# A four-layer graph network: TensorE's order given in the source, sums over features in quarters of columns, aggregation in 64x64 tiles

## The chip, the cores and the metric

The kernel runs on one core of one Trainium2 chip. A core has five engines with queues of their own: TensorE (PE in the profile, with its weight loads shown as PEld), VectorE (DVE), ScalarE (ACT), GpSimd (POOL) and SyncE (SP), which here only starts transfers. Matmul results land in PSUM, eight banks of 512 float32 values per partition; everything else lives in SBUF, 128 partitions wide. The metric is the device time of one execution in microseconds, the median of several runs.

## What is computed

The input x has 128 graphs of 64 nodes with 256 features, in float32. Four layers follow each other, each `x = layernorm(x + layer(x, adj))`:

```python
# layer 0: attention over the adjacency
Wh = x @ W
e = leaky(Wh @ a1 [:, None] + Wh @ a2 [None, :]);  e = -inf where adj == 0
out0 = softmax(e) @ Wh
# layer 1: attention over 512 edges (src, dst), 4 heads of 64 features
Xq, Xv = x @ W_lin.T, x @ W_val.T
e = einsum('behd,hd->beh', leaky_relu(Xq[:, src] + Xq[:, dst], 0.2), a) + log(A0[src, dst] + EPS)
attn = softmax of e over the edges with the same src
out1 = segment_sum(attn * Xv[:, dst], src) @ W_out.T
# layer 2: normalised adjacency, then two dense layers with batch norms
agg = A_hat @ x;  out2 = batchnorm(relu(batchnorm(agg @ W1.T + b1)) @ W2.T + b2)
# layer 3: two graph convolutions, then four LSTMs over windows of 1 to 4 nodes
```

Layers 0 and 1 and the first step of layer 2 (`agg`) are what the change touches.

## The kernel before

The 8192 rows (graph, node) are handled in sixteen blocks q of 512 rows, which is 8 graphs, or 4 columns c of 128 rows with 2 graphs (s) each. While block q is in the edge scores of layer 1, block q+2 is in layer 0, block q+1 is prepared for layer 1, and block q-3 gets its values, output projection and aggregation. Tiles in PSUM are `m` (three banks), `z` (two times two banks) and `e` (one bank).

The edge scores use leaky(t) = 0.2 t + 0.8 relu(t). The weights |a| are folded into the query weights, so that the sum over a head's features only has signs left. Per graph b of a block, one matmul pair z gathers query + query for all 512 edges (256 features in two halves of 128), ScalarE takes relu, VectorE adds the two halves (with a sign `same`, as the features are permuted so that both halves hold the same heads), and a matmul with the one-column-per-head matrix `apad` sums over features into 4 of the 128 rows of `e`:

```python
def reduce_heads(q, b, t):                                   # L312
    ...
    r0 = ((s * BPS + q % BPS) * PQ + c) * HEADS
    nc.tensor.matmul(pes[S], apad[:, P - HEADS - r0:2 * P - HEADS - r0], t, start=first, stop=False)

def l1_graph(q, b):
    c, s = divmod(b, 2)
    z = bank([KD, E], name="z", bufs=2)
    for k in range(KD):                                      # L322
        nc.tensor.matmul(z[:, k, :], L1[q]["qs"][c][:, s, k * P:(k + 1) * P], gath_r, start=True, stop=True)
    u = work.tile([P, KD, E], F32, name="u", bufs=4)
    nc.scalar.activation(u, z, AF.Relu)                      # L324
    nc.vector.scalar_tensor_tensor(u[:, 0, :], u[:, 1, :], same, u[:, 0, :], op0=OP.mult, op1=OP.add)  # L325
    pend.append((q, b, u[:, 0, :]))
    if len(pend) > DEEP:
        reduce_heads(*pend.pop(0))
```

Every second block, the softmax over edges runs on VectorE over the filled `e` (16 graphs x 4 heads in rows), with scans for the maximum and the sum per source node. Its result is scattered to a table in DRAM and read back (`ld`):

```python
def l1_softmax(S):
    nc.tensor.matmul(pe, spads[S % 2], gath, start=False, stop=True)                                 # L335
    nc.vector.tensor_add(e, pe, lb)
    nc.vector.tensor_tensor_scan(up, seg[:, :E], e, NEG, OP.add, OP.max)
    nc.vector.tensor_tensor_scan(dn[:, ::-1], seg[:, 1:][:, ::-1], e[:, ::-1], NEG, OP.add, OP.max)
    nc.vector.tensor_max(up, up, dn)
    nc.vector.tensor_sub(e, e, up)
    nc.scalar.activation(e, e, AF.Exp)
    ...  # two more scans; transposes of e and dn (L353); reciprocal (L357); weights at (L359); scatter; read back
```

Values, output projection and the aggregation for layer 2:

```python
def v_a(q):          # values: 64x64 tiles
    ...
    for c in range(PQ):
        for h in range(HEADS):
            for s in range(2):                               # L384
                nc.tensor.matmul(pY[s][r0:r0 + 64, h // 2, c, :], v[r, c, h * 64:(h + 1) * 64],
                                 am[r, c * HEADS + h, :], start=True, stop=True)
def v_b(q): ...      # output projection (L398), addition, layernorm into x2 on GpSimd, x2 to DRAM
def v_c(q):          # aggregation, with the block-diagonal matrix aht of two graphs
    for k in range(KD):
        p_ = bank([PQ, P])
        for c in range(PQ):                                  # L410
            nc.tensor.matmul(p_[:, c, :], x2[:, c, k * P:(k + 1) * P], aht, start=True, stop=True)
        nc.scalar.activation(A[:, q, k * QT:(k + 1) * QT], p_.rearrange("p c t -> p (c t)"), AF.Copy)
```

The loop names the steps in a rough order; what stands where on each engine is then settled by a scheduler that builds the program:

```python
for q in range(NQ):
    between = [
        [(l0_a, q + 2)],                      # transposes of x                (L201)
        [(l0_b, q + 2), (v_a, q - LAG)],      # layer 0's projection           (L222)
        [(l0_c, q + 2)],                      # scores, mask, exponentials     (L233, L236, L244)
        [(v_b, q - LAG), (l1_t, q + 1)],      # l1_t: transposes for layer 1   (L201)
        [(l1_qv, q + 1, 0), (l0_d, q + 2)],   # queries L287, values L290
        [],
        [(l1_qv, q + 1, 1), (v_c, q - LAG)],
        [(l0_e, q + 2)],                      # layer 0's aggregation (L263), layernorm
    ]
    for b in range(GQ):
        some(l1_graph, q, b)
        if q and q % BPS == 0 and b == DEEP - 1:
            l1_softmax(q // BPS - 1)
        for step, n, *more in between[b]:
            some(step, n, *more)
```

After the loop, the last three blocks' v_a, v_b and v_c alternate with layer 2's blocks (`up_block`, L684); layer 2's second dense layer is L749, layer 3's LSTMs are L927 and L933.

Of the kernel before, what the change touches and what calls it, by code (L numbers as in the profile page):

```python
# [17 lines left out]
P = 128  # L18
NB = 128
N = 64  # L20
# [11 lines left out]
SROWS = BPS * GQ * HEADS  # L32
PAIRS = N * N
# [7 lines left out]
def kernel(ctx: ExitStack, tc: tile.TileContext, i, out):  # L41
# [42 lines left out]
    def layernorm(dst, src, n, engine):  # L84
# [3 lines left out]
        ng = small.tile([P, n], F32, name="ln_ng", bufs=6)  # L88
        rs = small.tile([P, n], F32, name="ln_rs", bufs=6)
# [21 lines left out]
    with ExitStack() as two:  # L111
# [52 lines left out]
        for k in range(KD):  # L164
            for m in range(KD):
                nc.scalar.dma_start(
                    wq[:, k, m * P:(m + 1) * P].rearrange("p (h j) -> p h j", h=HEADS),
                    i["W_linT"][k * P:(k + 1) * P].rearrange("p (h m j) -> p m h j", h=HEADS, m=KD)[:, m])
        aL1 = su.tile([P, D], F32, name="aL1")
        for m in range(KD):  # L170
            nc.scalar.dma_start(aL1[:, m * P:(m + 1) * P].rearrange("p (h j) -> p h j", h=HEADS),
                              i["L1_gnn_a"].rearrange("h (m j) -> m h j", m=KD)[m].partition_broadcast(P))
# [4 lines left out]
        apad = wa.tile([P, 2 * P - HEADS], F32, name="apad")  # L177
        same = wa.tile([P, 1], F32, name="same")
# [37 lines left out]
        def l0_b(q):  # L216
# [10 lines left out]
            nc.gpsimd.tensor_copy(sb, wh[:, :, D + 1:].to_broadcast([P, PQ, P]))  # L227

        def l0_c(q):
# [4 lines left out]
            t = own(q, [P, PQ, P], "lr")  # L234
            for c in range(PQ):
                nc.vector.scalar_tensor_tensor(t[:, c, :], sc[:, c, :], wh[:, c, D:D + 1], mask,  # L236
                                               op0=OP.add, op1=OP.add)
            e = L0[q]["e"] = work.tile([P, PQ, P], F32, name="e0")
            nc.vector.scalar_tensor_tensor(e, t, SLOPE, t, op0=OP.mult, op1=OP.max)
# [40 lines left out]
        def l1_qv(q, c2):  # L280
            xT, v = L1[q]["xT"], L1[q]["v"]
            sp = spads[q // BPS % 2].rearrange("p (s b c h) -> p s b c h", s=4, b=BPS, c=PQ)
            pv = bank([2, D])
            for c in (2 * c2, 2 * c2 + 1):
# [10 lines left out]
                for s in range(2):  # L295
                    r, ro = slice(s * N, (s + 1) * N), slice((1 - s) * N, (2 - s) * N)
                    nc.scalar.activation(qs[r, s, :], pq[r, :D], AF.Copy)  # L297
                    nc.vector.tensor_sub(qs[ro, s, :], pq[r, :D], qs[r, s, :].bitcast(F32))  # L298
                    nc.scalar.activation(sp[r, s, q % BPS, c, :], pq[r, D:], AF.Copy, scale=SLOPE)
# [5 lines left out]
        def reduce_heads(q, b, t):  # L305
            S = q // BPS
            c, s = divmod(b, 2)
            r0 = ((s * BPS + q % BPS) * PQ + c) * HEADS
            first = q % BPS == 0 and b == 0
            if first:  # L310
                pes[S] = bank([E], name="e", bufs=1)
            nc.tensor.matmul(pes[S], apad[:, P - HEADS - r0:2 * P - HEADS - r0], t, start=first, stop=False)  # L312

        def l1_graph(q, b):

# [5 lines left out]
            u = work.tile([P, KD, E], F32, name="u", bufs=4)  # L323
            nc.scalar.activation(u, z, AF.Relu)  # L324
            nc.vector.scalar_tensor_tensor(u[:, 0, :], u[:, 1, :], same, u[:, 0, :], op0=OP.mult, op1=OP.add)  # L325
            pend.append((q, b, u[:, 0, :]))
            if len(pend) > DEEP:
                reduce_heads(*pend.pop(0))

        ld = {}  # L330

        def l1_softmax(S):
# [7 lines left out]
            nc.vector.tensor_tensor_scan(up, seg[:, :E], e, NEG, OP.add, OP.max)  # L340
            nc.vector.tensor_tensor_scan(dn[:, ::-1], seg[:, 1:][:, ::-1], e[:, ::-1], NEG, OP.add, OP.max)
            nc.vector.tensor_max(up, up, dn)
            nc.vector.tensor_sub(e, e, up)
            nc.scalar.activation(e, e, AF.Exp)


            nc.vector.tensor_tensor_scan(up, keep, e, 0.0, OP.mult, OP.add)
            nc.vector.tensor_tensor_scan(dn[:, ::-1], seg[:, 1:][:, ::-1], up[:, ::-1], NEG, OP.add, OP.max)
            rows = []
# [7 lines left out]
            nc.vector.reciprocal(rd, rows[1][:, :, :SROWS])  # L357
            for c in range(EC):
                nc.vector.scalar_tensor_tensor(at[:, c, :], rows[0][:, c, :SROWS], count[:, c:c + 1], rd[:, c, :],  # L359
                                               op0=OP.mult, op1=OP.mult)  # L360
# [11 lines left out]
        def v_a(q):  # L372
            S, b = divmod(q, BPS)
            v = L1[q]["v"]
            am = vp.tile([P, PQ * HEADS, N], F32, name="am", bufs=2)
            w = PQ * HEADS
            nc.gpsimd.tensor_copy(am, ld[S][:, :, b * w:(b + 1) * w].rearrange("p n r -> p r n"))
            pY = [bank([KD, PQ, N]) for _ in range(2)]
            for c in range(PQ):
                for h in range(HEADS):  # L380
                    for s in range(2):
# [3 lines left out]
                                         am[r, c * HEADS + h, :], start=True, stop=True)  # L385
# [4 lines left out]
        def v_b(q):  # L390
# [10 lines left out]
            x2 = L1[q]["x2"] = vp.tile([P, PQ, D], F32, name="x2")  # L401
# [3 lines left out]
        def v_c(q):  # L405
            x2 = L1.pop(q)["x2"]
            for k in range(KD):
                p_ = bank([PQ, P])
                for c in range(PQ):
                    nc.tensor.matmul(p_[:, c, :], x2[:, c, k * P:(k + 1) * P], aht, start=True, stop=True)  # L410
                nc.scalar.activation(A[:, q, k * QT:(k + 1) * QT], p_.rearrange("p c t -> p (c t)"), AF.Copy)
# [71 lines left out]
        acol = su.tile([P, KD], F32, name="acol")  # L483

        def setup_queries():

            tmp2 = su.tile([P, KD, D], F32, name="tmp2")
# [565 lines left out]
```

## Time and profile before

| | |
|---|---|
| time, median of 3 runs | 2237.45 us (2236.63 to 2239.74) |
| profiled execution | 2237.3 us, mean granted TensorE clock 0.991 |
| layers 0 and 1, with the start | about 0 to 610 us |
| layer 2 (dense layers) | about 610 to 850 us |
| layer 3 | about 850 us to the end |
| e matmuls (L312) | 133.1 us busy, 256 instructions |
| z matmuls (L322) | 106.9 us busy, 256 instructions |
| combination of halves on VectorE (L325) | 106.3 us busy, 128 instructions |
| aggregation for layer 2 (L410) | 33.9 us busy, 256 instructions |

A float32 matmul of the program is two instructions in the trace. TensorE's instructions overlap each other, so that one lasts longer in the trace than the distance to the next start; the distances of starts tell how fast TensorE works, and its busy time is the time covered by at least one instruction. The row of a group gives the count, the busy time, the mean length of one in ns, and the idle time ahead of them with what ended it.

### The profile page before, as it was taken

The page shows a single profiled execution, that of the slowest core. Times are in us where ns is not written, and L with a number is a line of the kernel's source. Part 1 is how long each engine was busy: PE and PEld are TensorE (multiplying, and loading weights), DVE is VectorE, ACT ScalarE, POOL GpSimd, SP SyncE. Part 2 cuts the span into 40 slices and gives each one's busy share as a digit, 9 for nine tenths or more (in the row PEclk, how much of TensorE's full clock was granted, in tenths as well). Part 3 has the DMA queues.
Part 4 walks back from the last instruction along what each step waited for, and adds up shares of the span by engine and source line. Part 5 has one row for each costly group of instructions (what it writes and reads, how often), then busy time and mean ns, then how long its engine had stood idle before and what let it go on. Part 6 is the DMA issues. An engine that isn't in the chain of part 4 may idle for free.

```text
span 2237.3 us, 27559 instructions
## 1 busy us (share of the span) xinstructions
PE 2163.4 (97%) x10675; PEld 1411.7 (63%) x10675; DVE 926.0 (41%) x2136; ACT 944.6 (42%) x1821; POOL 435.0 (19%) x561
## 2 busy tenths in 40 slices
PE   5989999999899998999999999999999999999998
PEld 4667676666554444468468468468468468568467
DVE  7576756666544435232232323323323323323212
ACT  2655665656334802343343333333433433433333
POOL 1133334333320002011111111112112112112002
PEclk8999999999999998999999999999999999999999
DMA  4021233202223003000000000001001001000001
GB/s 121 19 40 29 50 50 51 50 32 39 41 41 111 19 0 104 0 20 29 29 20 29 29 19 29 29 20 29 29 19 29 28 20 29 19 10 29 10 0 29
DMA packets 129266, 74.46 MB, mean 33 GB/s; under 512 B 84976, under 2 KB 119920, under 8 KB 128880
## 3 DMA queue, kind: packets, MB, share of 16 engines
q1 hardware_dynamic: 124528, 70.74, 13.0%
q8 instruction: 84, 1.38, 0.3%
q10 hardware_dynamic: 3584, 0.92, 0.2%
q0 software_dynamic: 1024, 1.05, 0.2%
q14 instruction: 46, 0.38, 0.1%
HBM read 44.12 MB, written 28.57 MB: 32 GB/s over the span
## 4 chain that ended last, share of the span: by engine, by line
PE 81%; DVE 9%; ACT 5%; POOL 2%; DMA 1%; issue 1%; ACTq 0%; SPq 0%; POOLq 0%; DVEq 0%
PE l L927 34%; PE l L933 19%; PE pz L749 5%; PE pz L684 4%; DVE u L325 3%; PE g L867 2%; PE g L879 2%; PE e L312 2%; PE m L287 2%; PE m L222 2%; PE m L398 1%; PE g L829 1%; ACT u L324 1%; PE m L410 1%; PE m L290 1%
## 5 line engine op out<-in xcount | busy, mean ns | idle before, releaser
L927 PE MATMUL l<-H,wih 128*128 128x256 f32 (+2 forms) x2496 | 792.7, 470 | 0.8 <-ACT gate_g L947 0.5
L927 PEld LDWEIGHTS l<-H,wih 128*128 128x128 f32 x2496 | 467.7, 190 | 273.7 <-issue 179.4
L933 PE MATMUL l<-hid,whh 128*128 128x256 f32 (+2 forms) x1536 | 435.9, 437 | 0.0
L933 PEld LDWEIGHTS l<-hid,whh 128*128 128x128 f32 x1536 | 291.9, 190 | 128.4 <-issue 61.2
L939 ACT ACTIVATE gate_i<-l,bias 128x256 f32<-128x256 f32 (+2 forms) x176 | 100.0, 568 | 522.7 <-PE l L933 468.7
L942 DVE TENSOR_TENSOR gate_i<-gate_i,gate_g 128x256 f32<-128x256 f32 (+2 forms) x96 | 47.8, 498 | 580.8 <-ACT gate_g L939 580.8
L943 POOL TENSOR_TENSOR cell<-gate_f,cell 128x256 f32<-128x256 f32 (+2 forms) x96 | 83.6, 871 | 903.8 <-ACT gate_f L939 903.8
L82 POOL TENSOR_TENSOR ln_rs<-ln_rs,mhalf 128x2 f32<-128x2 f32 (+2 forms) x97 | 79.5, 819 | 498.7 <-DVE ln_ng L94 497.6
L324 ACT ACTIVATE u<-z 128x1024 f32<-128x1024 f32 x128 | 129.5, 1024 | 59.4 <-PE z L322 58.8
L312 PE MATMUL e<-u,apad 128*128 128x512 f32 x256 | 133.1, 606 | 11.3 <-DVE u L325 9.9
L939 ACT ACTIVATE gate_g<-l,bias 128x256 f32<-128x256 f32 (+2 forms) x176 | 100.1, 569 | 99.1 <-PE l L927 49.9
L325 DVE SCALAR_TENSOR_TENSOR u<-u,same 128x512 f32<-128x512 f32 x128 | 106.3, 841 | 57.8 <-ACT u L324 56.9
L939 ACT ACTIVATE gate_o<-l,bias 128x256 f32<-128x256 f32 (+2 forms) x176 | 99.2, 564 | 64.1 <-PE l L933 54.1
L946 DVE TENSOR_TENSOR cell<-gate_i,gate_g 128x512 f32<-128x512 f32 (+2 forms) x80 | 48.3, 603 | 156.1 <-ACT gate_g L939 155.6
L947 ACT ACTIVATE gate_g<-cell 128x256 f32<-128x256 f32 (+2 forms) x176 | 89.9, 511 | 52.9 <-DVE cell L946 38.4
L684 PE MATMUL pz<-A,w 128*128 128x512 f32 x256 | 112.1, 594 | 0.0
L322 PE MATMUL z<-gath_r,qs 128*128 128x512 f32 x256 | 106.9, 499 | 0.5 <-DVE qs L298 0.3
L684 PEld LDWEIGHTS pz<-A,w 128*128 128x128 f32 x256 | 48.1, 190 | 56.4 <-issue 54.3
L952 DVE TENSOR_TENSOR H<-gate_o,gate_g 128x512 f32<-128x512 f32 (+1 forms) x64 | 40.9, 639 | 89.0 <-PE l L927 71.4
L298 DVE TENSOR_TENSOR qs<-m,qs 64x256 fp32r<-64x256 f32 x128 | 54.1, 423 | 54.9 <-ACT qs L297 53.3
L939 ACT ACTIVATE gate_f<-l,bias 128x256 f32<-128x256 f32 (+2 forms) x96 | 51.0, 531 | 59.7 <-PE l L933 59.7
L287 PE MATMUL m<-wq,tT 128*128 128x260 f32 x256 | 71.2, 396 | 3.7 <-ACT tT L202 3.2
(240 smaller groups left out, 2674.8 us busy)
## 6 DMA issues: line engine op xcount, KB each, us to landing
xin<-in_x SPq DMA_DIRECT2D x16, 512.0 KB
ld<-table SPq DMA_DIRECT2D x16, 512.0 KB
x_dram<-x SPq DMA_DIRECT2D x16, 512.0 KB
x2r<-x_dram SPq DMA_DIRECT2D x32, 256.0 KB
x_dram<-A SPq DMA_DIRECT2D x64, 128.0 KB
x3r<-x_dram SPq DMA_DIRECT2D x64, 128.0 KB
out<-st SPq DMA_DIRECT2D x64, 128.0 KB
wih<-in_WihT SPq DMA_DIRECT2D x3, 1024.0 KB
```

The lines of the kernel that those rows point to most:

```text
L287: nc.tensor.matmul(pq, xT[:, k, c * P:(c + 1) * P], wq[:, k, :], start=k == 0, stop=k == KD - 1)
L312: nc.tensor.matmul(pes[S], apad[:, P - HEADS - r0:2 * P - HEADS - r0], t, start=first, stop=False)
L322: nc.tensor.matmul(z[:, k, :], L1[q]["qs"][c][:, s, k * P:(k + 1) * P], gath_r, start=True, stop=True)
L324: nc.scalar.activation(u, z, AF.Relu)
L325: nc.vector.scalar_tensor_tensor(u[:, 0, :], u[:, 1, :], same, u[:, 0, :], op0=OP.mult, op1=OP.add)
L684: nc.tensor.matmul(p_, w1[:, k, m * P:(m + 1) * P], A[:, q, k * QT:(k + 1) * QT], start=k == 0, stop=k == KD - 1)
L749: nc.tensor.matmul(p_, w2[:, k, m * P:(m + 1) * P], hidden(q, k), start=k == 0, stop=k == M1 - 1)
L927: nc.tensor.matmul(gates[n], wih[p][:, k, mw * P:(mw + 1) * P], Hw[:, k, :, s, :], start=k == 0, stop=not s and k == KD - 1)
L933: nc.tensor.matmul(gates[n], whh[p][:, k, m * P:(m + 1) * P], hid[:, k], start=False, stop=k == KD - 1)
L939: nc.scalar.activation(act[n], gates[n], AF.Tanh if n == "g" else AF.Sigmoid, bias=bias[:, p - 1, m:m + 1])
L943: nc.gpsimd.tensor_tensor(cell[:, j], act["f"], cell[:, j], OP.mult)
L947: nc.scalar.activation(act["g"], cell[:, j], AF.Tanh)
```

## The change

It does four things in layers 0 and 1, and one small thing at the start of layer 3.

- The sums over features no longer need VectorE's combination. `apad` now holds 32 columns for each half, and the sum of one graph is two accumulating matmuls (one per half) of 32 output rows. Four graphs go together, each in its own quarter of TensorE's columns and of `e`'s rows. The features are no longer permuted, so the query weights and the vector a come in plain order.
- The aggregation for layer 2 uses 64x64 tiles, one per graph and 64 features, and leaves out the zero blocks of `aht`; inside the loop it writes both halves into one `z` tile, which ScalarE copies out at once.
- The order of TensorE's steps is given in the source: each step's TensorE instructions are queued behind the last of the step before. The softmax is cut into three steps; the lag of v_b and v_c grows by one block.
- Smaller things: the second maximum scan starts from the first's result, so that a separate maximum is gone; the spread `sb` moves from GpSimd to ScalarE; layernorm's two factors share a tile; layer 0's scores and the residual sum are updated in place; `u` has seven buffers; after the loop eleven steps, not nine, alternate with layer 2's blocks; the two halves of layer 3's first group take their first two steps one half after the other.

```diff
-        for k in range(KD):
-            for m in range(KD):
-                nc.scalar.dma_start(
-                    wq[:, k, m * P:(m + 1) * P].rearrange("p (h j) -> p h j", h=HEADS),
-                    i["W_linT"][k * P:(k + 1) * P].rearrange("p (h m j) -> p m h j", h=HEADS, m=KD)[:, m])
+        nc.scalar.dma_start(wq[:, :, :D], i["W_linT"].rearrange("(k p) c -> p k c", p=P))
 ...
-            nc.gpsimd.tensor_copy(sb, wh[:, :, D + 1:].to_broadcast([P, PQ, P]))
+            nc.scalar.activation(sb, wh[:, :, D + 1:].to_broadcast([P, PQ, P]), AF.Copy)
 ...
-        def reduce_heads(q, b, t):
+        def reduce_heads(four):
+            q, b, _ = four[0]
 ...
-            nc.tensor.matmul(pes[S], apad[:, P - HEADS - r0:2 * P - HEADS - r0], t, start=first, stop=False)
+            for k in range(KD):
+                for q, b, u in reversed(four):
+                    n, r0 = b % 2 * 2 + b // 2 % 2, (q % BPS * 2 + b // 4) * HEADS
+                    nc.tensor.matmul(pes[S][n * CG:(n + 1) * CG, :],
+                                     apad[:, k, CG - HEADS - r0:2 * CG - HEADS - r0], u[:, k, :],
+                                     start=r0 == 0 and k == 0, stop=False)
 ...
-            u = work.tile([P, KD, E], F32, name="u", bufs=4)
+            u = work.tile([P, KD, E], F32, name="u", bufs=7)
             nc.scalar.activation(u, z, AF.Relu)
-            nc.vector.scalar_tensor_tensor(u[:, 0, :], u[:, 1, :], same, u[:, 0, :], op0=OP.mult, op1=OP.add)
 ...
-            nc.vector.tensor_tensor_scan(dn[:, ::-1], seg[:, 1:][:, ::-1], e[:, ::-1], NEG, OP.add, OP.max)
-            nc.vector.tensor_max(up, up, dn)
-            nc.vector.tensor_sub(e, e, up)
+            nc.vector.tensor_tensor_scan(dn[:, ::-1], seg[:, 1:][:, ::-1], up[:, ::-1], NEG, OP.add, OP.max)
+            nc.vector.tensor_sub(e, e, dn)
 ...
-        def v_c(q):
+        def v_c(q, one=True):
 ...
+            for c in range(PQ):
+                for k in range(KD):
+                    for h in range(2):
+                        for s in range(2):
+                            r, f = slice(s * N, (s + 1) * N), slice(h * 64, (h + 1) * 64)
+                            nc.tensor.matmul(p_[s][f, k, c, :], x2[r, c, k * P + h * 64:k * P + (h + 1) * 64],
+                                             aht[r, r], start=True, stop=True)
 ...
+        def step(do, n, *more):
 ...
+                with tc.issue_after(queue[-1]):
+                    do(n, *more)
 ...
+            mine = [t for t in traced[first:] if t.engine == mybir.EngineType.PE]
+            queue.extend(mine[-1:])
 ...
             between = [
-                [(l0_a, q + 2)],
-                [(l0_b, q + 2), (v_a, q - LAG)],
-                [(l0_c, q + 2)],
-                [(v_b, q - LAG), (l1_t, q + 1)],
-                [(l1_qv, q + 1, 0), (l0_d, q + 2)],
-                [],
-                [(l1_qv, q + 1, 1), (v_c, q - LAG)],
-                [(l0_e, q + 2)],
+                [(l0_e, q + 1), (l0_a, q + 2)],
+                [(sums, q if q else -1), (l1_softmax, S)],
+                [(l1_sums, S), (l0_b, q + 2)],
+                [(v_b, q - LAG - 1)],
+                [(l1_weights, S), (l1_t, q + 1), (l0_c, q + 2)],
+                [(sums, q), (l1_qv, q + 1, 0)],
+                [(v_c, q - LAG - 1), (v_a, q - LAG)],
+                [(l0_d, q + 2), (l1_qv, q + 1, 1)],
             ]
```

## The prediction

> **What bounds the kernel now.** I read the busy times first, then a table by stage, then the chain, the waits and the timeline of TensorE inside one repeat of layers 0 and 1. One "step" is one q of the loop over sixteen blocks of 512 rows; two steps share one edge softmax, so the work repeats every two steps.
>
> ```profile
> PE 2163.4 (97%) x10675; PEld 1411.7 (63%) x10675; DVE 926.0 (41%) x2136; ACT 944.6 (42%) x1821; POOL 435.0 (19%) x561
> ```
>
> TensorE looks full over the whole span, everybody else half empty. The stage table of one two-step repeat says the same of the loop (columns: time; busy us and instructions of PE, weight loads, DVE, ACT, POOL; granted clock; DMA share; GB/s):
>
> ```profile
> 281.10:351.90 70.80, 68.42 (x427) 49.93 (x426) 46.94 (x110) 42.92 (x95) 26.05 (x28) 1.00 0.27 47
> ```
>
> But 68.4 of 70.8 us is not all work. The chain gives lengths of stretches of matmuls that follow each other without waiting (start, length, what, count):
>
> ```profile
> 323.31 0.86 PE e L312 x2
> 324.17 0.88 PE m L287 x4
> 325.04 0.86 PE m L290 x4
> ...
> 327.64 1.87 PE m L410 x16
> 329.52 0.46 PE z L322 x2
> ...
> 330.84 1.73 PE m L263 x8
> ...
> 349.37 2.63 PE m L222 x12
> ...
> 354.65 3.45 PE m L398 x16
> ```
>
> From these one step's TensorE work is: z 8 x 0.47 = 3.8; e 8 x 0.86 = 6.9; queries 4 x 0.88 = 3.5; values 4 x 0.86 = 3.4; layer 0's projection 16/12 x 2.63 = 3.5; its aggregation 1.7; output projection 3.45; aggregation for layer 2 1.87; value aggregation 1.2 (timeline below); 24 transposes at about 0.11 = 2.7; half of the softmax's own matmuls and transposes 0.9. Sum 32.9 us, 65.8 us for two steps. The period is 70.8 to 71.1 us (the softmax matmul L335 stands at 265.13, 335.93, 406.86 and 477.95), so 5.1 us per two steps are waiting, more than the row of idle time shows. The timeline shows where it hides:
>
> ```profile
> 339.21 0.19 PEld L322 LDWEIGHTS z<-gath_r,qs 128*128 128x128 f32 x1 [0.24 <-issue]
> 339.23 1.03 PE L322 MATMUL z<-gath_r,qs 128*128 128x512 f32 x2
> ...
> 340.08 0.81 DVE L325 SCALAR_TENSOR_TENSOR u<-u,same 128x512 f32<-128x512 f32 x1
> ...
> 340.95 1.13 PE L312 MATMUL e<-u,apad 128*128 128x512 f32 x2 [0.68 <-DVE u L325]
> ```
>
> The z pair is drawn as 1.03 us though it takes 0.47, and the e pair behind it waits for VectorE's combination, which is queued behind the softmax scans on VectorE. So the loop is bound by TensorE's work, with VectorE's combination ending most waits.
>
> **What the Trainium skill says.** "Perfetto Trace Analysis", section "Tensor Engine Instruction (MATMUL, LD_WEIGHTS)", says TensorE's end times are computed from the instruction's size, not observed; the 1.03 beside 0.47 agrees, hence my use of starts. "TensorE: Matmul & The Clock Gate", section "Part 3: Packing small matmuls — row/col tiling", says matmuls in distinct column groups run at the same time, and lists 2.38x for three 32-column tiles of 512. No run here shows 32-column tiles yet. The kernel does have 64x64 tiles:
>
> ```profile
> 351.91 1.16 PE L384 MATMUL m<-am,v 64*64 64x64 f32 x64
> ```
>
> A float32 instruction of 512 columns starts every 0.43 us (0.86 for a pair), so one of 64 columns should take 0.053, and 64 of them 3.4 us one after the other. They take 1.16 us including the drain: the four tiles do run together. "TensorEngine Tiling (Array Packing)", section "Key Properties", says that changing the tiling mode drains the array. The trace has it: from the last projection matmul L222 to the first L384 matmul 0.31 us pass where 0.22 are usual, and 0.15 us pass after the last tile; I count 0.1 us at either end.
>
> **The change, part by part.**
>
> Sums over features (e). Before, each of 128 graph blocks took one VectorE combination (106.3 us busy in all) and one full-width matmul, 0.86 us. After, the combination is gone and each block has two matmuls of 32 output columns; four blocks stand in four column groups, eight matmuls together. If four run side by side, eight need 2 x 0.86 = 1.72 us, plus 0.2 for the two drains: 1.92 against 4 x 0.86 = 3.44. Saved 1.52 x 2 = 3.0 us per step.
>
> Aggregation for layer 2. Sixteen full-width instructions of 1.87 us become 64 instructions on 64x64 tiles, the same form as L384: 1.2 us with the drains. Saved 0.67 us per step.
>
> TensorE's work per step is then 32.9 - 3.0 - 0.7 = 29.2 us, 58.4 per two steps.
>
> Waits. VectorE loses 12.7 us of its 46.9 per repeat (the L325 row of that window) and one 0.68 us maximum, so it has 33.5 us of work; ScalarE's 42.9 stays about (it gains the 0.6 us spread of sb from GpSimd per step and loses 0.2 in the aggregation's copy). Against some 62 us neither is a bound by load. But TensorE now goes in source order, and I followed two steps through the built order by hand. In the step with a softmax, VectorE's queue after the scans holds the y additions, eight statistics, the 1.75 us reciprocal and the at products before layer 0's scores; TensorE's transposes of the scores need the bank that the reciprocal reads, about 1.3 us late. The two transposes of l1_t use one bank there, so the second waits for ScalarE's 0.6 us copy. Layer 0's four exponentials stand in ScalarE's queue ahead of most query copies, and the value aggregation then waits about 1 us for its bank. In the other step I find about 1 us. So some 4.2 us of waits stay per two steps, against 5.1.
>
> Loop: two steps take 58.4 + 4.2 = 62.6 us instead of 70.9; 8.3 us saved, times 8 = 66 us.
>
> Outside the steady loop. (1) Start: the query weights come in one transfer of whole rows instead of four of 128-byte pieces; the chain now waits until 12.9 us for them and the vector behind them, and two products and reductions leave VectorE's setup: I take 4 us. (2) End of the loop, 588 to 612 us: matmul starts there account for only about 15 us of work in 24, because e waits 4.2 us for the combination and the aggregation waits for the normalisation on GpSimd (2.74 us) and the scans. With the combination gone and two more steps interleaved with layer 2's blocks I take 7 us. (3) Layer 3's first group goes half by half: 1.5 us of the 8 us before its first aggregation. Layers 2 and 3 otherwise keep their work: 0.
>
> Sum: 66 + 4 + 7 + 1.5 = 78.5, so 2237 - 79 = 2158 us.
>
> **Rivals.**
>
> (a) The column tiles do not overlap four ways. Then eight matmuls take 3.4 us at two ways or 6.9 at none, and e costs the same or 7 us more per step. For it: four streams over the full 128 rows have no case in this trace, and every float32 matmul is two instructions on the same tile, which might hold up the next tile. Against it: L384 has the same two instructions per matmul, two column groups per row group, and still 3.4/0.94 = 3.6 ways between its first and last start. At two ways the gain shrinks to waits, the aggregation and the edges: about 2205. At none: about 2320.
>
> (b) The waits take the saving back: a fixed order cannot pass a late operand, and ScalarE at about 43.5 us of 62 is the fullest helper with long queues. If each repeat loses 8 us instead of 4.2, the time is about 2190.
>
> (c) The order works as intended and almost all waits go: 1 us per two steps, 26 us more saved, with the start a little better: about 2130.
>
> (d) Nothing in the tail or the start changes because those stretches wait for transfers (the 10.3 us read of the table, ld, after 628 us): 2158 + 12 = 2170.
>
> **Range and chances.** The middle is the sum, 2158. Rivals (c) and (b) set the ends, 2135 and 2192. Two per cent faster is 2192.7; of the rivals only (a) lies beyond, which I give one in eight. Faster by over 2% 0.86, within 2% 0.11, slower by over 2% 0.03.
>
> **What would show it right or wrong.** Four-way tiles: eight e instructions in a stretch should start within about 1.7 us, sixteen instruction records per block with starts in fours some 0.43 us apart; starts 0.43 apart one by one prove rival (a). The aggregation's 64 instructions should span 0.94 us. The softmax matmul should repeat every 62 to 63 us; 58 to 60 means (c), above 66 means (b). Waits should name ScalarE's copies (v, tT, qs) and VectorE's reciprocal, no longer the combination. From the first L749 matmul (738.9 us) to the end the kernel now takes 1498 us; that should shrink by 1.5 us, and if it moves by more than 4, something that I did not see is at work.

## The result, and the profile after

The changed kernel takes 2182.18 us (median of 4 runs, 2181.03 to 2183.27), against 2238.59 us for the kernel before beside it (2236.63 to 2240.04). The ratio is 0.9748, with a 95% interval of 0.9732 to 0.9765: 2.5% faster, a gain of 56 us where 79 were forecast. Line numbers moved with the edit: the sums over features are now L311, z L320, relu L322, the softmax matmul L330, its row transposes L354, the aggregation for layer 2 L421, value aggregation L387, output projection L401, queries and values L283 and L286, transposes L197, scores L229.

The first row of the page after (busy us, share of the span, instructions):

```profile
PE 2106.3 (97%) x11699; PEld 1368.9 (63%) x11699; DVE 821.3 (38%) x1995; ACT 945.5 (43%) x1825; POOL 403.2 (18%) x545
```

TensorE is as "full" as before, with 57 us less in it; VectorE has 105 us less, since the combinations are gone; the shares alone say nothing of the gain. The table by stage of the kernel after (time; busy us and instructions of PE, weight loads, DVE, ACT, POOL; clock; DMA share; GB/s) shows where it came from: from the first z matmul to the first softmax, one steady repeat, and the last repeat:

```profile
49.00:116.40 67.40, 61.00 (x300) 41.17 (x298) 27.06 (x85) 48.61 (x108) 7.37 (x12) 0.95 0.05 16
...
302.90:366.50 63.60, 60.42 (x558) 44.55 (x554) 34.83 (x93) 42.83 (x95) 22.11 (x27) 1.00 0.29 53
...
494.10:542.70 48.60, 42.05 (x435) 26.26 (x431) 19.56 (x48) 24.98 (x41) 19.80 (x21) 0.89 0.29 47
```

The last repeat of the kernel before, in the same view:

```profile
548.00:594.40 46.40, 42.13 (x272) 26.13 (x270) 30.96 (x53) 23.78 (x40) 19.38 (x16) 1.00 0.25 38
```

The steady repeat went from 70.9 to 63.65 us, much as forecast. The last one became longer, with a mean granted clock of 0.89. By the starts of the softmax matmul (eight of them) the whole difference of the two profiled spans, -55.8 us, divides like this:

| stretch | before | after | difference |
|---|---|---|---|
| start to the first z matmul | 54.5 | 49.3 | -5.2 |
| first z to first softmax | 67.3 | 67.2 | -0.1 |
| six repeats, first to seventh softmax | 426.2 | 377.7 | -48.5 |
| seventh to eighth softmax | 46.4 | 48.6 | +2.2 |
| eighth softmax to the first matmul of the second dense layer | 144.5 | 139.8 | -4.7 |
| from there to the end | 1498.4 | 1499.0 | +0.6 |

Of the six repeats the first two gave 12.8 and 7.8 us, the others 6.1 to 7.4. The chain of the kernel after in a steady repeat (start, length, what, count; stretches of matmuls that follow each other without waiting):

```profile
334.51 0.47 PE z L320 x2
334.98 1.85 PE e L311 x16
336.83 0.67 PE z L320 x2
337.50 3.49 PE m L218 x16
340.99 0.47 PE z L320 x2
341.45 3.45 PE m L401 x16
```

One block of four graphs takes 1.85 us where four matmuls of 0.86 stood; z (0.47), the projection (3.49) and the output projection (3.45) are what they were. The list of waits over three repeats (engine, line, waited for: us in all, times, longest) names other things than before:

```profile
PE m L283 <- ACT yT L391: 3.3, 6, 0.6
PE m L197 <- ACT tT L198: 2.1, 3, 0.7
PE m L197 <- DVE y L403: 1.7, 3, 0.6
PE m L229 <- DVE ln_mv L93: 1.3, 3, 0.4
```

VectorE's combination, first in the same list of the kernel before (2.1 us in three waits), is gone from it. In TensorE's timeline (start, length, line, tiles and shapes, count, idle time before and its releaser) the three lower ones are seen in the step with a softmax, and the first behind the two blocks of 64x64 tiles:

```profile
313.79 0.63 PE L197 MATMUL m<-ident,A 128*128 128x128 f32 x4 [0.58 <-DVE y L403]
315.11 0.66 PE L197 MATMUL m<-ident,A 128*128 128x128 f32 x4 [0.69 <-ACT tT L198]
316.21 0.66 PE L229 MATMUL m<-ident,sb 128*128 128x128 f32 x4 [0.45 <-DVE ln_mv L93]
...
323.26 1.16 PE L421 MATMUL z<-aht,y 64*64 64x64 f32 x64
324.24 1.15 PE L387 MATMUL m<-am,v 64*64 64x64 f32 x64
325.41 0.73 PE L320 MATMUL z<-gath_r,qs 128*128 128x512 f32 x2
325.98 0.60 PE L248 MATMUL m<-ident,e 128*128 128x128 f32 x4
327.14 1.14 PE L283 MATMUL m<-wq,tT 128*128 128x260 f32 x4 [0.56 <-ACT yT L391]
```

The distances of starts show more than the idle times in brackets: four transposes take 0.44 us when they follow each other, but from 313.79 to 315.11 it is 1.32, and L248 stands for 1.16. Summed up in this way a repeat has about 57.7 us of TensorE's work and 5.9 us of waits, an estimate from these distances.

One thing the busy time doesn't show is TensorE's clock. From the first z matmul to the last softmax the trace of the changed kernel has 30.7 us at half the full clock, in six stretches: 6.8 ahead of the first softmax, 13.7 in the six repeats and 10.2 in the last repeat. The kernel before has 6.8 us there (3.4 ahead of the first softmax, 3.4 in the six repeats, none in the last). If TensorE sets the pace all through such a stretch, half of it is lost, so the change lost at most 12 us of its gain in this way; this is an estimate.

### The profile page after: what moved, and what is told of

Read it like the earlier page. It is cut to its first block, busy times and chain, and to the rows that moved or that the text cites. A ratio compares the mean times of both kernels' runs of the same rounds, so it can differ in the third digit from the quotient of the medians.

```text
span 2181.5 us, 29360 instructions
## 1 busy us (share of the span) xinstructions
PE 2106.3 (97%) x11699; PEld 1368.9 (63%) x11699; DVE 821.3 (38%) x1995; ACT 945.5 (43%) x1825; POOL 403.2 (18%) x545
## 4 chain that ended last, share of the span: by engine, by line
PE 86%; ACT 5%; DVE 5%; issue 2%; POOL 1%; DMA 0%; POOLq 0%; SPq 0%; DVEq 0%; ACTq 0%
PE l L950 35%; PE l L956 19%; PE pz L772 5%; PE pz L707 5%; PE e L311 3%; PE g L890 2%; PE g L902 2%; PE m L283 2%; PE m L218 2%; PE m L286 1%; PE g L852 1%; PE z L320 1%; PE m L401 1%; ACT u L322 1%; PE m L197 1%
## 5 line engine op out<-in xcount | busy, mean ns | idle before, releaser
L322 ACT ACTIVATE u<-z 128x1024 f32<-128x1024 f32 x128 | 130.4, 1026 | 57.9 <-PE z L320 56.9
L320 PE MATMUL z<-gath_r,qs 128*128 128x512 f32 x256 | 100.0, 479 | 0.6 <-ACT u L322 0.4
L283 PE MATMUL m<-wq,tT 128*128 128x260 f32 x256 | 71.8, 404 | 7.6 <-ACT yT L391 5.4
L865 ACT ACTIVATE st<-A,sh,sc 128x256 f32<-128x256 f32 x64 | 34.4, 588 | 84.1 <-DVE sh L692 78.9
L311 PE MATMUL e<-u,apad 128*32 128x512 f32 x512 | 67.0, 644 | 1.2 <-ACT u L322 1.2
```

The lines of the kernel that those rows point to most:

```text
L283: nc.tensor.matmul(pq, xT[:, k, c * P:(c + 1) * P], wq[:, k, :], start=k == 0, stop=k == KD - 1)
L311: nc.tensor.matmul(pes[S][n * CG:(n + 1) * CG, :], apad[:, k, CG - HEADS - r0:2 * CG - HEADS - r0], u[:, k, :], start=r0 == 0 and k == 0, ...
```

## The experiments

Theory: the column tiles alone make the gain, the new order keeps waits from eating it, and the 20-odd us that are missing were lost at the two edges of the loop, where TensorE's work does not set the pace. Rivals: the order or the 64x64 aggregation carries part of the gain; the tiles depend on the order of instructions; the fixed order itself costs time in the loop. Softmax starts were read in each trace, as in the table above; differences between kernels come from the same stretches.

### e1: tiles alone

The tiles stay, and so do the smaller changes; the steps stand in the old rough order, the scheduler is free, the lag is the old one, and nine steps follow the loop.

```diff
-            if queue:
+            if False:
 ...
-                [(l0_e, q + 1), (l0_a, q + 2)],
-                [(sums, q if q else -1), (l1_softmax, S)],
-                [(l1_sums, S), (l0_b, q + 2)],
 ...
+                [(l0_a, q + 2)],
+                [(sums, q if q else -1), (l1_softmax, S), (l1_sums, S), (l1_weights, S), (l0_b, q + 2), (v_a, q - LAG)],
+                [(l0_c, q + 2)],
 ...
```

> The changed kernel with the old list of steps (v_a, v_b, v_c, l0_e and the softmax where they stood, nine tail steps) and the scheduler free again; the sums in quarters, the 64x64 aggregation and the small changes stay. Theory (the gain is TensorE's work taken out by the tiles): most of the gain stays, 2178 to 2200 us, two steps still repeat in under 66 us. Rival (the gain is the order given in the source, which removes waits): at least half of the gain is lost, 2210 us or more, and two steps repeat in 68 us or more.

Measured: 2195.03 us (2194.3 to 2195.7), ratio 0.98 (0.9783 to 0.9816); repeat 65.2 us, last repeat 58.0. So the tiles, together with the smaller changes, which were not tried by themselves, bring 45 of the 56 us without any given order, and the rest of the change 11 to 13 us. By stretches e1's span of 2192.9 us is 11.4 longer than the changed kernel's: 9.7 in the six repeats, 9.4 in the last, less 4.0 up to the first softmax and 3.7 after the loop.

### e2: the old sums in the new order

Order, lag and 64x64 aggregation stay; VectorE's combination and one full-width matmul per graph come back, with the permuted weights that they need, and `u` has six buffers for lack of room.

```diff
-            for k in range(KD):
-                for q, b, u in reversed(four):
-                    n, r0 = b % 2 * 2 + b // 2 % 2, (q % BPS * 2 + b // 4) * HEADS
-                    nc.tensor.matmul(pes[S][n * CG:(n + 1) * CG, :], ...
+            for q, b, u in four:
+                c, s = divmod(b, 2)
+                r0 = ((s * BPS + q % BPS) * PQ + c) * HEADS
+                nc.tensor.matmul(pes[S], apad[:, P - HEADS - r0:2 * P - HEADS - r0], u, ...
 ...
+            nc.vector.scalar_tensor_tensor(u[:, 0, :], u[:, 1, :], same, u[:, 0, :], op0=OP.mult, op1=OP.add)
```

> The changed kernel with its order and its 64x64 aggregation, but the sums over features as before: VectorE adds the two halves and one full-width matmul per graph sums over features, four graphs in a row (u has six buffers). Theory (tiles): a block of four takes 3.4 us instead of 1.85, 32 blocks, so 2182 + 51 = 2233 us, and two steps repeat in 70 us. Rival (order): the order keeps most of the gain, 2205 us or less.

Measured: 2244.37 us (20 runs), ratio 1.0018 (1.0012 to 1.0025); repeat 71.7 us. By stretches its profiled span is 4.7 us longer than that of the kernel before: 2.3 up to the first z matmul, 4.9 from there to the first softmax and 7.2 in the last repeat, less 5.1 in the six repeats and 4.8 after the last softmax. A stretch of 3.41 us at half the clock lies in each steady repeat, so that some 1.7 us of the 71.7 are not the order's own; from the first z matmul to the last softmax there are 41.0 us of such stretches, where the kernel before has 6.8. So without the tiles the order, the aggregation and the smaller changes gain nothing as measured. What they would gain at full clock is not shown: by the estimate of half a stretch it is at most some 12 us.

### e3: half by half

The two loops of a block exchanged: both halves of a graph, which go to the same quarter of columns, follow each other in the program.

```diff
-            for k in range(KD):
-                for q, b, u in reversed(four):
+            for q, b, u in reversed(four):
+                for k in range(KD):
```

> The changed kernel with the two loops of the sums exchanged: both halves of one graph, that is two matmuls and four instructions on the same quarter of columns, follow each other before the next quarter's. Theory (instructions wait for their own quarter only): a block still takes 1.85 us and the time stays at 2182 us within 6. Rival (TensorE starts matmuls strictly in the order of the program, so only neighbours in different quarters overlap): a block takes (16 - 3) x 0.43 = 5.6 us, and the time is about 2182 + 32 x 3.7 = 2300 us.

Measured in one run: 2182.26 us. A block still takes 1.35 us from its first to its last start and 0.52 to what follows; its sixteen instructions still start in fours, 13 ns apart within a four and 0.43 us from four to four (at 336.28, 336.74, 337.17 us). In the changed kernel the four starts are 6.5 ns apart. The doubled distance fits twice as many instructions standing between one quarter's first and the next quarter's, so the order did change; but the trace names no quarter, and that the four of a group belong to four quarters is inferred. What is shown is that for blocks of this size the order of the source does not matter for the time.

### e4: the same sums at full width

Each of the eight matmuls of a block writes all 128 rows; the other columns of `apad` are zero, and `u` has six buffers.

```diff
-        apad = wa.tile([P, KD, 2 * CG - HEADS], F32, name="apad")
+        apad = wa.tile([P, KD, 2 * P - HEADS], F32, name="apad")
 ...
-                    nc.tensor.matmul(pes[S][n * CG:(n + 1) * CG, :],
-                                     apad[:, k, CG - HEADS - r0:2 * CG - HEADS - r0], u[:, k, :],
+                    nc.tensor.matmul(pes[S], apad[:, k, P - HEADS - n * CG - r0:2 * P - HEADS - n * CG - r0], u[:, k, :],
```

> The changed kernel with the same eight matmuls per block, but each over all 128 columns (a wider apad, zero outside the graph's four rows; u has six buffers); no combination on VectorE. Theory (the quarters run four at a time): a block takes 8 x 0.86 = 6.9 us instead of 1.85, so 2182 + 32 x 5.0 = 2343 us. Rival (the gain is that VectorE's combination is gone, the width matters less): under 2250 us.

Measured in one run: 2315.49 us; repeat 81.9 us. The chain of this kernel:

```profile
300.26 0.47 PE z L319 x2
300.73 6.87 PE e L311 x16
307.60 0.88 PE m L283 x4
```

A block takes 6.87 us at full width and 1.85 in quarters, 3.7 times less, with what the change of tile size costs at both ends in it. That is the cost that the prediction gave rival (a) without any overlap, with about 2320 us for the whole. "TensorE: Matmul & The Clock Gate", section "Part 3: Packing small matmuls — row/col tiling", gives a speedup of 2.38 for three tiles of 32 columns and no figure for four; per tile this trace does better (3.7 of 4 against 2.38 of 3). Thirty-two blocks of 5.0 us more are 161 us, but the kernel is only 133 us longer: with more work in TensorE the helpers are done in time and waits shrink (the longest for `yT` falls from 0.6 to 0.3 us), and from the first z matmul to the last softmax 6.8 us at half clock stand where the changed kernel has 30.7, worth up to 12 us by the estimate above.

### e5: the binding removed

The new list of steps stays, but TensorE's instructions are not tied to each other; the scheduler may reorder.

```diff
-            if queue:
+            if False:
                 with tc.issue_after(queue[-1]):
```

> The changed kernel with its new list of steps, but TensorE's order is left to the scheduler again (no step is queued behind the one before). In the program built so, most of a repeat stands in the same order; it differs in the first steps and around the softmax. Theory (the new list does it, not the binding): within 8 us of 2182. Rival (the binding does it): 2192 us or more, near the 2195 of the old list.

Measured: 2175.53 us (2172.94 to 2175.78), ratio 0.9716 (0.97 to 0.9733); repeat 63.1 us, last repeat 46.5. With the binding, which gave the change its name, the kernel takes 6.7 us more; what helps is the new list of steps and the lag. Against e1, where the scheduler is free too, the new list, the lag and the two more steps after the loop bring 19.5 us. Of the difference of the two profiled spans, 8.0 us, 6.6 lie in the six repeats and 2.0 in the last, less 0.6 elsewhere. A steady repeat without halved clock is only 0.55 us shorter, 3.3 in six; the stretches at half clock fall from 30.7 to 17.1 us, worth up to 7. How much is the order's own and how much the clock's is not separated.

### e6: the aggregation for layer 2 at full width

```diff
-                            nc.tensor.matmul(p_[s][f, k, c, :], x2[r, c, k * P + h * 64:k * P + (h + 1) * 64],
-                                             aht[r, r], start=True, stop=True)
+            for k in range(KD):
+                for c in range(PQ):
+                    nc.tensor.matmul(p_[k][:, c, :], x2[:, c, k * P:(k + 1) * P], aht, start=True, stop=True)
```

> The changed kernel with the aggregation for layer 2 in full-width matmuls, as before. Theory (TensorE's work counts in full): a block takes 1.87 us instead of 0.98, so 16 x 0.9 = 14 us and a little for the drains, 2195 to 2199 us; two steps repeat in 65.5 us. Rival (it lies where TensorE waits anyway): 2182 within 4.

Measured: 2181.08 us (2179.75 to 2181.8), ratio 0.9744 (0.9727 to 0.976): the same as with 64x64 tiles; its first repeat without a stretch of halved clock takes 63.66 us. The timeline of this kernel, at the place shown above:

```profile
322.78 0.73 PE L320 MATMUL z<-gath_r,qs 128*128 128x512 f32 x2
323.35 0.60 PE L248 MATMUL m<-ident,e 128*128 128x128 f32 x4
323.79 1.15 PE L283 MATMUL m<-wq,tT 128*128 128x260 f32 x4
```

The queries now follow L248 after 0.44 us, with no wait for `yT`. The two aggregations together take 0.8 us longer (1.88 and 1.09 against 0.98 and 1.17), and the queries behind them wait 0.7 less. In the loop the tiles were real work saved, and all of it went into a wait for ScalarE. After the loop it is otherwise: there e6 takes 2.0 us longer from the last softmax to the second dense layer. That the totals agree even so goes with fewer stretches at half clock (20.5 us instead of 30.7).

### e7: the softmax rows in z

The eight transposes of the softmax's rows (L354) go to the two banks of a z tile instead of two of the three `m` banks.

```diff
-            for row in (e, dn):
-                p_ = bank([EC, P])
+            if one:
+                both = bank([2, E], name="z", bufs=2)
+            for j, row in enumerate((e, dn)):
+                p_ = both[:, j, :].rearrange("p (c t) -> p c t", c=EC) if one else bank([EC, P])
```

> The changed kernel, but the eight transposes behind the edge softmax go to a z tile instead of two of the three m banks. Theory (TensorE's waits there come from the three m banks: l1_t waits for the y addition and for ScalarE's copy of the same bank, the scores for the reciprocal): some 1.5 to 2.5 us less per two steps and fewer stretches at half clock behind it, 2165 to 2175 us; two steps repeat in about 62 us. Rival (the operands are late themselves): 2182 within 4.

Measured: 2173.16 us (2172.25 to 2174.34), ratio 0.9708 (0.9692 to 0.9724); repeat 62.5 us. The rows and the layer's eight transposes behind them now follow each other densely (0.87 us for eight transposes, where the two groups took 1.62 and 2.42); the waits of L197 for `y` and `tT` are gone from the list of waits. Of these 2.3 us half comes back, as a steady repeat is 1.1 us shorter: a wait of L248 for ScalarE's `spad`, at most 0.8 us, and one of the value aggregation for `v`, at most 0.6 us, are new. So 1.1 us of a repeat's waits came from the rotation of three banks, not from the work of any engine. Six repeats of this are 6.6 of the 9.0 us gained; the stretches at half clock are fewer here as well (20.5 us).

### e8: the end of the loop

The last step's aggregation for block 11 and values for block 12 move behind the loop; the two halves of layer 3's first group alternate as before the change.

```diff
-                [(v_c, q - LAG - 1), (v_a, q - LAG)],
+                [(v_c, q - LAG - 1), (v_a, q - LAG)] if q < NQ - 1 else [],
 ...
-        for do, n in [(v_b, NQ - LAG - 1), (v_c, NQ - LAG - 1)] + [
+        for do, n in [(v_c, NQ - LAG - 2), (v_a, NQ - LAG - 1), (v_b, NQ - LAG - 1), (v_c, NQ - LAG - 1)] + [
 ...
-            for half in [0, 0, 1, 1] + [0, 1] * (GCN_STEPS - 2):
+            for half in [0, 1] * GCN_STEPS:
```

> Two edits at places that the trace tells apart. At the end of the loop: the last step's aggregation (block 11) and values (block 12) move behind the loop, between layer 2's blocks. At the start of layer 3: the two halves of the first group alternate again, as before the change. Theory for the first (in the last two steps TensorE waits behind the normalisation on GpSimd in a fixed order, about 11 of 48.6 us, and then the clock halves): the last two steps take 42 to 45 us and the total falls by 4 to 8 us. Rival: the wait only moves behind the loop, total within 2 us. For the second: from layer 2's last matmul to the first LSTM matmul 36.6 us now; theory (the same normalisation ends both orders): within 1 us; rival (half by half is better): 1.5 us longer.

Measured: 2176.91 us (2175.8 to 2178.52), ratio 0.9728 (0.9712 to 0.9744); last repeat 42.5 us instead of 48.6, and 140.7 to the second dense layer instead of 139.8; 5.3 us in all. Why the two steps hurt there is in the chain of the changed kernel, just ahead of the last softmax:

```profile
531.16 2.16 POOL y L97 x4
533.32 1.89 POOL am L379
535.25 1.69 PE m L387 x64
...
539.26 3.50 PE e L311 x16
542.77 1.07 PE e L330 x2
```

TensorE's fixed order stands behind GpSimd, which normalises block 11 and then copies the values' matrix `am`, 4 us; only after that come the last two graphs and the sums that the softmax needs. And behind these waits the last block of sums takes 3.50 us instead of 1.85, at half the clock (from 535.7 us for 6.83 us).

Layer 3's start did not move: from the last matmul of the second dense layer to the first LSTM matmul 36.45 us here, 36.6 with the order of the change and 36.6 in the kernel before. The order of the halves is worth nothing.

### e9: the values in z

The value aggregation too goes to a z tile, in order to free `m` banks.

```diff
-            pY = [bank([KD, PQ, N]) for _ in range(2)]
+            if one:
+                both = bank([2, E], name="z", bufs=2)
+                pY = [both[:, s, :].rearrange("p (k c n) -> p k c n", k=KD, c=PQ) for s in range(2)]
```

> The changed kernel, but the value aggregation writes into one z tile instead of two of the three m banks. In the changed kernel the queries behind it wait 0.7 us per step for ScalarE's copy of those banks, which stands behind the copy of layer 2's aggregation. Theory (that wait eats what the 64x64 aggregation saves, 0.8 us per step): most of it comes back, some 0.4 us after a new wait for z, 13 steps: 2173 to 2179 us. Rival (the wait moves to z, which ScalarE empties as late): 2182 within 3.

Measured: 2184.85 us (2184.38 to 2185.7), ratio 0.9763 (0.9747 to 0.978). No gain. The list of waits of this kernel over the same three repeats:

```profile
PE z L391 <- ACT u L322: 5.7, 6, 1.0
PE m L197 <- ACT tT L198: 2.1, 3, 0.7
PE m L197 <- DVE y L407: 1.7, 3, 0.6
```

The queries' wait for `yT`, 3.3 us, has become a wait of 5.7 us, ahead of the value aggregation, for relu's copies out of the z tiles. At this place ScalarE is late with either bank.

### e10, e11 and e12: together

The scheduler free, softmax rows in z and the end of the loop as above (the order of the halves as in the change):

> The changed kernel with three edits together: the scheduler free, the softmax's transposes in z, the end of the loop as in e8. One by one they gave 6.7, 9.0 and 5.3 us. Theory (they remove different waits): 2162 to 2166 us. Rival (the first two remove the same waits around the softmax): 2168 to 2172 us.

Measured: 2166.19 us (2165.4 to 2169.3), ratio 0.9682 (0.9666 to 0.9698). The three gains of 6.7, 9.0 and 5.3 us would add up to 21; 16 came, between the theory and the rival. The last repeat takes 38.6 us.

The same with the values in z and the preparation of the adjacency in two parts, the second four graphs later, so that TensorE's steps don't wait for a power (an inverse square root) that GpSimd takes in it:

```diff
+            adj.extend((an, deg, dd))
+
+        adj = []
+
+        def setup_adjacency2():
+            an, deg, dd = adj
             ph_ = bank([P])
 ...
-        setup += [setup_place, setup_adjacency]
+        setup += [setup_place, setup_adjacency] + [lambda: None] * 3 + [setup_adjacency2]
```

> The same with two more edits: the value aggregation in z, and the adjacency's setup cut in two, the second part four places later. The second should take the wait of 3.4 us and the stretch at half clock near 90 us out of the start: 3 to 5 us. With the values in z 5 us more: 2153 to 2160 us. If one of the two does nothing or costs something: 2160 to 2168 us.

Measured: 2166.54 us (2163.13 to 2168.52), ratio 0.9676 (0.966 to 0.9692): no change in the sum, but two opposite ones in the trace. The first softmax comes 5.2 us earlier (111.9 against 117.1 in e10), the six repeats lose 4.8 us and the last one 2.0, with the values in z and two stretches at half clock in the six (e10 has none there). The stage table of the changed kernel near 90 us, and then of e11:

```profile
85.00:88.50 3.50, 1.48 (x12) 0.52 (x4) 0.31 (x2) 1.02 (x1) 3.40 (x6) 1.00 0.00 0
88.50:95.30 6.80, 6.07 (x16) 4.99 (x17) 0.83 (x3) 0.77 (x2) 0.26 (x1) 0.50 0.27 77
```

```profile
85.00:88.50 3.50, 3.50 (x26) 1.73 (x25) 2.29 (x13) 1.60 (x4) 1.37 (x2) 1.00 0.00 0
88.50:95.30 6.80, 6.80 (x44) 5.11 (x46) 1.71 (x6) 5.36 (x11) 2.32 (x5) 1.00 0.28 81
```

In the changed kernel TensorE is busy for 1.48 of 3.5 us while GpSimd works (3.40), and the next 6.8 us run at half the clock. In e11 TensorE is busy throughout, and the clock stays at 1.00: with the wait gone, the halved clock is gone too.

The last version is e10 with the adjacency in two parts, and the values where they were:

> The kernel of e10 (scheduler free, softmax's transposes in z, end of the loop moved) with the adjacency's setup cut in two, and without the values in z, which cost in e9. Theory (the setup's wait and its stretch at half clock are worth 5 us, and e11 hid them behind the loss of the values in z): 2159 to 2163 us, the first softmax matmul near 112 us instead of 117. Rival (later stretches at half clock fall elsewhere and take it back): 2164 to 2168 us.

Measured: 2162.40 us (5 runs, 2162.02 to 2163.01), ratio 0.9653 (0.9639 to 0.9666). It is the best of all, 20 us below the changed kernel. Its stage table, two steady repeats and the last:

```profile
291.80:355.10 63.30, 60.70 (x558) 44.85 (x554) 35.77 (x93) 42.86 (x95) 22.54 (x27) 1.00 0.30 53
355.10:417.70 62.60, 60.50 (x559) 44.77 (x555) 34.73 (x93) 42.87 (x95) 22.68 (x27) 1.00 0.27 54
479.00:519.10 40.10, 35.88 (x306) 22.90 (x302) 19.52 (x48) 22.77 (x38) 17.95 (x20) 0.96 0.34 55
```

Against the changed kernel its span is 20.3 us shorter: 5.0 up to the first softmax (at 111.4 instead of 116.5), 10.1 in the six repeats, 8.4 in the last repeat, and 3.3 longer after the loop, where the moved steps are. Part of this is the clock: 6.7 us at half clock are left of 30.7.

## Why the prediction was right and wrong

**Faster by over two per cent, and inside the range; but the sum was 23 us too large.** 2182 lies inside 2135 to 2192, near its upper end.

**Four-way tiles: right.** 1.92 us for a block was forecast, 1.85 measured, in fours 0.43 us apart as the sign said. The 1.85 us, beside 6.87 at full width, rule rival (a) out.

**The steady repeat: nearly right, in part by luck, as two errors offset each other.** 62.6 us forecast, 63.65 measured. TensorE's work was about 57.7 us, not 58.4: two neighbouring blocks of 64x64 tiles show no drain between them (0.04 us from the last L421 to the first L387). Waits were 5.9 us, not 4.2. The term mis-sized is "some 4.2 us of waits stay per two steps". The second transpose's wait for ScalarE's copy was as foreseen (0.69 us). The wait for the scores' bank was named as 1.3 us behind the reciprocal; it measured 0.45 behind the layernorm's statistics. The value aggregation's wait of 1 us did not come, but one for `yT` at the queries did, twice a repeat, as well as one for the residual addition's bank (0.58 us). Rival (b), with 8 us, was the direction, at about half of its excess.

**"Aggregation: saved 0.67 us per step": failed.** TensorE's time in it fell by 0.9 us, but the full-width experiment has the same repeat and the same total. I counted every removed microsecond of TensorE as time, though the next instruction there waits for ScalarE. In the steady repeat this cost was hidden before it was removed; after the loop it did count (2.0 us). The values in z show that ScalarE remains late at that place with another bank too.

**"8.3 us saved, times 8 = 66": the largest error.** Only six of the eight repeats are steady. These gave 48.5 us, 8.1 each on average, but 7.25 in the steady state. The first one (to the first softmax) gave 0.1 and the last became 2.2 us longer: 16.6 us forecast, -2.1 measured, and with the six repeats 1.3 us short of 49.8 this is 20 of the 23 us missing. Ahead of the first softmax TensorE waits for the preparation of the adjacency and then runs at half clock; taking that wait out brings the first softmax forward by 5 us (e11, e12). At the end of the loop the fixed order stands behind GpSimd's normalisation; moving two steps shortens the last repeat by 6.0 us and the whole by 5.3 (e8). The profile of the kernel before had the sign: its last repeat had 42.1 of 46.4 us busy, where the steady one had 68.4 of 70.8, and I multiplied by the number of repeats without a row for it. The sum also had no term for TensorE's clock: by the estimate above at most 12 us were lost to more stretches at half clock, up to 1.7 ahead of the first softmax, 5 in the six repeats and 5 in the last. How much of the 23 us this is, was tried only near 90 us (e11, e12).

**The edges.** Start: 4 us forecast, 5.2 measured, right. In e2, which has the old query weights and their preparation again, the first z matmul stands at 56.8 us (54.5 before, 49.3 after), which fits the reason given; transfers and preparation were not told apart. End of the loop: 7 forecast; after the last softmax 4.7 came, and the last repeat gave 2.2 back. Forecast was a gain from the combination's end and two more steps there; the wait for GpSimd ahead of the last softmax, in the fixed order, was not. Layer 3's first group: 1.5 us forecast, none came (0.6 longer from the first matmul of the second dense layer to the end), and e8 shows the order of the halves without effect. Rival (d) was right for layer 3 only.

**What the order does.** The prediction took the fixed order as a part of the mechanism. The runs divide it: list, lag and binding together are worth some 12 us behind the tiles; without the tiles nothing was gained as measured, at a clock that was more often halved. Behind the tiles the list, the lag and two more steps after the loop bring 19.5, and the binding, with the clock that came with it, takes 6.7 back. Rival (c), where the order removes almost all waits, is out: even the best version keeps a repeat of 62.6 us with about 57.7 of work.

## What to carry to other kernels

A saving per repeat holds for the repeats that look like the one you measured: give the first and last a stage row of their own before you multiply, and ask there which engine is late. Work taken from the fullest engine counts only if the next instruction on it is not already waiting for another; taking the saving out again (as with the full-width aggregation) shows that in one run. And a better list of steps and a binding of the order are two changes: try the list with the scheduler free.

## What the runs showed of the hardware

Four column quarters of 32 work side by side, and the order of the source within a block did not matter: with the loops exchanged the starts still came in fours, and the time stayed at 2182.26 us. Eight matmuls of 512 float32 columns took 1.85 us together and 6.87 us one after the other.

In these traces TensorE's clock is halved in stretches of 3.41 us or a small multiple (6.83, 10.24, 13.65, 17.07). From the first z matmul to the last softmax the changed kernel had 30.7 us of them, the kernel before 6.8, and the best version (e12) 6.7. A layer 0 projection that fell into one took 5.94 us instead of 3.49. "TensorE: Matmul & The Clock Gate", section "Part 1: The HAM clock gate (the "warmup" mystery)", says that the clock is gated to half after an idle window of about 3.4 us, and that the windows run freely. The lengths agree. The waits here were shorter than a window: in the 3.5 us ahead of each of the changed kernel's six stretches TensorE was still busy for 1.2 to 1.8 us, 1.48 ahead of the one at 88.5 us. That one went when its wait went (e11, e12). Elsewhere it was only seen, not tried, what brings them: without the binding 17.1 us were left (e5), but the full-width sums, bound as well, had 6.8 (e4). Where they fall shifts with every edit: the full-width aggregation had one in two of its repeats (65.3 instead of 63.7 us). With the old sums in the new order one came in five successive repeats of 71.7 us, which is 21 times 3.41. A part of what the other runs gain or lose in the loop, perhaps 1.6 us for a stretch of 3.41, is of this kind and not of their edits.
